# Edge network: some source rows fetched one by one on SyncE's queue, more columns copied on VectorE and ScalarE

## The chip, the cores and the metric

The kernel runs on one core of one Trainium2 chip. A core has five engines that run their own instruction streams: TensorE (PE in the profile, with its weight loads as PEld), VectorE (DVE), ScalarE (ACT), GpSimd (POOL) and SyncE (SP). Each has a sequencer that reads its stream in order, waits on semaphores and hands work to the engine; PEq, SPq and so on in the profile are these sequencers. DMAs are issued by SP, ACT or POOL and run on 16 shared DMA engines. SBUF is on-chip memory of 128 partitions, PSUM is where TensorE writes.

The metric is device time in microseconds (us). The kernel before takes 1879.1 us, the median of three runs (1875.58 to 1879.48).

## The reference

A graph has 12500 nodes with 64 features, and 212500 edges sorted by their destination, each with 32 features of its own. One layer computes a message for each edge from source, destination and edge features, sums messages by destination, updates the nodes and normalises:

```
msg_in = concatenate([nodes[src], nodes[dst], edge_features], axis=-1)   # 64 + 64 + 32
messages = relu(msg_in @ mW1 + mb1) @ mW2 + mb2                          # hidden size 128
aggregated = segment_sum(messages, dst, num_segments=12500)
upd_in = concatenate([nodes, aggregated], axis=-1)
update = relu(upd_in @ uW1 + ub1) @ uW2 + ub2
out = layernorm(nodes + update)
```

Everything is float32. The features of the source nodes must be fetched by index, in no order; the destinations of neighbouring edges lie close together.

## The kernel before, in words

**Groups and steps.** The edges are cut into tiles of 128 (P), and three tiles (TG) make a group; there are 554 groups (G). The main loop makes one step for each group k, numbered 0 to 553. One step's TensorE work is software-pipelined over groups: the transposes of group k (`turn`, L378), the hidden product of group k - 2 (`hidden`, L404) and the sums of group k - 4 (`sums`, L431, and every fourth step the counts, L442). In the last ten steps (SHORT) these stand in steps of their own. The first of TensorE's instructions in a step carries all the waits of the step.

**How the source features come in.** There are two ways.

- *Gathered.* `gather` (L164 to L175) issues on POOL one indirect DMA for each tile. It brings 128 rows of x (64 numbers each) to the 128 partitions of a tile in a ring `own.s` of 20 groups (RING). It is called 16 groups ahead (AHEAD), and waits until the group that used the ring's place before has been transposed. TensorE turns the tile over (`turn`), and ScalarE copies the result from PSUM to the matrix `own_st` (L389).
- *Copied as columns.* The kernel also holds x transposed in SBUF (`xc`, one column for each node). For the first tile of some groups (`COPIED`) nothing is gathered. Instead VectorE and ScalarE copy one column after another from `xc` to `own_st`, at an address that comes from a register (`fetch`, L565 on VectorE and L567 on ScalarE, 64 partitions by 4 bytes). From step 18 (BEGIN) to step 543 each step copies 44 columns: on VectorE 12 and 8 (VCOLS), on ScalarE 12 and 12 (ACOLS). Each such part is preceded by a load of its addresses into registers (`registers`, L546, a TENSOR_LOAD on the engine's own sequencer). The addresses come to SBUF eight steps at a time (`indexes`, L525, on SP), and VectorE scales them (`addresses`, L531). Where a tile is copied, ScalarE's copy from PSUM is in two pieces.

**The other work of a step.** VectorE takes the maximum with zero of the hidden product (L415), adds the sums into a window of 32 nodes of `agg` (L458, at an address from a register) and every fourth step the counts (L463), and writes the one-hot placement of a later group (`onehot`, L366). SP loads, for each group, a window of 32 projected destination rows as part of the hidden product's weights (`window`, L358, at a register address, four groups ahead), for each four groups the edge features (`inputs`, L316), and writes finished output (L516). In the first 25 steps parts of x and of the projected table also pass (L225, L226, L340 to L344). About every 22 steps a block of 512 nodes is complete, and its update runs in six pieces spread over following steps (L474 to L511).

**What sets the order.** The order of instructions on each engine is that of the program as written; no planner moves them. In a step, VectorE's first load of registers is recorded ahead of the addition L458, by a small list: `between.append(lambda: registers(k, 0))` before the step, and in `add`, `if between: between.pop()()`. Then come the step's additions, `fetch(0)` (the first part's columns), `window`, `onehot`, and for each later part its `registers` and `fetch`, and last the gather of group k + 16. Each DMA on SP uses one of eight semaphores in turn, and an instruction that reuses a semaphore waits for the DMA that had it before.

Of the kernel before, what the change touches and what calls it, by code (L numbers as in the profile page):

```python
# [10 lines left out]
F32 = mybir.dt.float32  # L11
BF16 = mybir.dt.bfloat16
I32 = mybir.dt.int32
# [3 lines left out]
ET = mybir.EngineType  # L17
# [15 lines left out]
G = (E + GE - 1) // GE  # L33
SB = 4
AHEAD = 16
RING = AHEAD + 4
BLOCKS = 3
NW = 2 * SB
COUNT = 96
# [9 lines left out]
TIMES = 4  # L49
BEGIN = 18  # L50
CHECKED = 8
VCOLS = (12, 8)
ACOLS = (12, 12)
COLS = sum(VCOLS + ACOLS)
SPAN = 8


def tiles_of(g):

    n = min(GE, E - g * GE)  # L60
    return [min(P, n - j * P) for j in range((n + P - 1) // P)]
# [23 lines left out]
COPIED = []  # L85
while BEGIN - (-P * (len(COPIED) + 1) // COLS) < G - SHORT:
    COPIED.append(BEGIN - (-P * (len(COPIED) + 1) // COLS))


class Own:  # L90
# [24 lines left out]
def ordered(ctx: ExitStack, tc: tile.TileContext, a, own, ok):  # L115
# [21 lines left out]

    loads, places_by, copy_by, relu_by, sums_by, wm_by, turn_by = ({} for _ in range(7))
    efs_by, hidden_by, counted_by = {}, {}, {}
    columned = set(COPIED)  # L140

    def after(first, *others):

# [20 lines left out]
    def gather(g):  # L164
        s = own.s[g % RING]
        loads[g] = [
            nc.gpsimd.indirect_dma_start(  # L167
                out=s[:p, j, :D], out_offset=None, in_=x[:, :],
                in_offset=bass.IndirectOffsetOnAxis(
                    ap=src_sb[:p, g * TG + j : g * TG + j + 1], axis=0),  # L170
            )
            for j, p in enumerate(tiles_of(g)) if j or g not in columned
        ]
        for i in loads[g]:
            after(i, *([turn_by[g - RING]] if g >= RING else []))  # L175

# [93 lines left out]
    wc = const.tile([H, H], F32, name="wc")  # L270

    starts, rows_at, indices, columns_by = {}, {}, {}, {}
    by_dst = dram.tile([NP, H], F32, name="by_dst")
    written = []

# [9 lines left out]

    def ordered_edges():

        off = temp.tile([P, G * TG], F32, name="off")
        valid = temp.tile([P, 2], F32, name="valid")
        nc.vector.tensor_scalar(off, dlc, 0.0, 0.0, ALU.is_ge, ALU.add, accum_out=valid[:, 0:1])  # L290
        nc.vector.tensor_scalar(off, dlc, W - 1.0, 0.0, ALU.is_le, ALU.add, accum_out=valid[:, 1:2])
        low = temp.tile([1, G], F32, name="low")
        opens = [0, *(closes for *_, closes in PLAN)]
        for (base, *_), g0, g1 in zip([*PLAN, (N,)], opens, [*opens[1:], G]):
            if g0 < g1:
                nc.vector.memset(low[:, g0:g1], float(base))
        wrong = temp.tile([1, 2, G], F32, name="wrong")
        nwrong = temp.tile([1, 1], F32, name="nwrong")
        first_f = temp.tile([1, G], F32, name="first_f")
        nc.vector.tensor_copy(first_f, first_i[0:1, :])  # L300
        nc.vector.tensor_tensor(wrong[:, 0], first_f, low, ALU.is_lt)
        nc.vector.tensor_tensor(wrong[:, 1], first_f, high, ALU.is_gt)
        nc.vector.tensor_reduce(nwrong, wrong, mybir.AxisListType.XY, ALU.add)
        vps = ups.tile([H, CH], F32, name="u_ps")
        for i in range(2):
            nc.tensor.matmul(vps[0:1, 0:1], ones[:, 0:1], valid[:, i : i + 1], start=i == 0,
                             stop=i == 1)
        nv = temp.tile([1, 1], F32, name="nv")
        nc.vector.tensor_tensor(nv, vps[0:1, 0:1], nwrong, ALU.subtract)
        nc.vector.tensor_scalar(ok, nv, float(E + P * G * TG), None, ALU.is_equal)  # L310
# [52 lines left out]
    def onehot(g):  # L363
        if g >= G:
            return
        places_by[g] = nc.vector.tensor_tensor(  # L366
            own.s[g % RING][:, :, D:], iota.unsqueeze(1).to_broadcast([P, TG, W]),
            dlc[:, g * TG : (g + 1) * TG].unsqueeze(2).to_broadcast([P, TG, W]), ALU.is_equal,
        )
        after(places_by[g], *([counted_by[g - RING]] if g >= RING else []))  # L370

    def turn(g, ps):


        s = own.s[g % RING]
        xt = ps[0][: D + W, :GE]
        did = [
            nc.tensor.transpose(xt[:, j * P : j * P + p], s[:p, j, :], ident[:p, :p])  # L378
            for j, p in enumerate(tiles_of(g))
        ]  # L380

        def copy(step):
            t, c, n = columns(g)
            turn_by[g] = step
            whole = [(slice(D + W), slice(n))]
            apart = [(slice(D, D + W), slice(P)), (slice(D + W), slice(P, n))]
            copies = [
                ordered_by_steps(
                    after(nc.scalar.activation(t[r, c : c + n][:, m], xt[r, m], AF.Copy), step))  # L389
                for r, m in (apart if g in columned else whole)  # L390
            ]
            if g >= BLOCKS * SB:
                after(copies[0], hidden_by[g - BLOCKS * SB])
            copy_by[g] = copies
            return copies

        return did, [*loads.pop(g), places_by[g]], copy

    def hidden(g, ps):
        t, c, n = columns(g)  # L400
# [24 lines left out]
    def sums(g, ps):  # L425
        h, s = own.h[g % NH], own.s[g % RING]
        sizes = tiles_of(g)
        sg = ps[2][:, : TIMES * W].rearrange("p (t w) -> p t w", w=W)
        did = []
        for j, p in enumerate(sizes):  # L430
            did.append(nc.tensor.matmul(  # L431
                sg, h[:p, j, :],
                s[:p, j, D:].unsqueeze(1).to_broadcast([p, TIMES, W]),
                start=j == 0, stop=j == len(sizes) - 1))
        counts = []
        if g % SB == SB - 1 or g == G - 1:
            g0 = g // SB * SB
            whole = [q for q in range(g0, g + 1) if tiles_of(q) == [P] * TG]
            at_ps = ps[2][0:1, TIMES * W :][:, : SB * W].rearrange("o (q w) -> o q w", w=W)
            first_s = g0 % RING  # L440
            for j in range(TG):
                did.append(nc.tensor.matmul(  # L442
                    at_ps[:, : len(whole)], own.one,
                    own.ring[:, first_s : first_s + len(whole), j, D:],
                    start=j == 0, stop=j == TG - 1))
            if len(whole) < g + 1 - g0:
                for j, p in enumerate(sizes):
                    did.append(nc.tensor.matmul(
                        at_ps[:, len(whole)], own.one[:p], s[:p, j, D:],
                        start=j == 0, stop=j == len(sizes) - 1))  # L450
            counts = [(q, at_ps[:, q - g0]) for q in range(g0, g + 1)]

        def add(step):
            sums_by[g] = step
            at = bass.ds(starts[g], W)
            if between:
                between.pop()()
            did = [after(nc.vector.tensor_tensor(agg[:, at], sg[:, 0, :], agg[:, at], ALU.add),  # L458
                         step)]
            for q, counted in counts:  # L460
                counted_by[q] = step
                count = xc[COUNT : COUNT + 1, bass.ds(starts.pop(q), W)]
                did.append(after(nc.vector.tensor_tensor(count, counted, count, ALU.add), step))  # L463
            return did

        return did, [*relu_by[g], *copy_by[g]], add
# [53 lines left out]
    def indexes(i):  # L520

        n = min(SPAN * COLS, P * len(COPIED) - i * SPAN * COLS)
        if n > 0:
            indices[i] = ixp.tile([1, SPAN * COLS], I32, name="index")
            nc.sync.dma_start(indices[i][:, :n], a["src_copied"][:, i * SPAN * COLS :][:, :n])  # L525
# [27 lines left out]
    def fetch(*parts):  # L553

        for part in parts:
            engine, c0, v = held.pop(part, (None, 0, ()))
            for q, at in enumerate(v, c0):
# [8 lines left out]
                else:  # L566
                    by[engine] = nc.scalar.activation(o, x_at, AF.Copy)  # L567
                ordered_by_steps(after(by[engine],
                                       *([hidden_by[g - BLOCKS * SB]] if new else [])))

    waiting = [(closes, update(base, p, n)) for base, p, n, closes in PLAN]
    now = []

# [37 lines left out]
    for g in range(SB):  # L611
        window(g)
    indexes(0)
    made = summed = 0
    between, held = [], {}

    for k in range(G):
        if k < BITS:
# [11 lines left out]
        if k % SB == 1:  # L630
            places(k // SB + 1)
        if k < G - SHORT:
            between.append(lambda: registers(k, 0))
            step((turn, k), *([(hidden, k - 2)] if k > 1 else []),
                 *([(sums, k - 4)] if k > 3 else []))
            made, summed = max(0, k - 1), max(0, k - 3)
            if between:
                between.pop()()
            fetch(0)
        else:  # L640

            step((turn, k))
            for _ in range(2):
                if summed < made:
                    step((sums, summed))
                    summed += 1
            for _ in range(2):
                if made <= k:
                    step((hidden, made))
                    made += 1  # L650
        window(k + SB)
        onehot(k + LEAD)
        if k < G - SHORT:
            for part in range(1, len(VCOLS + ACOLS)):
# [338 lines left out]
```

## Time and profile before

| | |
|---|---|
| median of three runs | 1879.1 us (1875.58 to 1879.48) |
| profiled execution: its own time | 1872.44 us |
| its span in the profile | 1870.6 us |
| granted TensorE clock, mean | 0.952 |
| busy: ACT, DVE, POOL, PE | 1558.7, 1452.9, 1400.1, 1302.0 us |
| gathers on POOL (L167) | 1481, mean 945 ns |
| columns on ACT (L567), on DVE (L565) | 12560, 10480 |
| DMAs of SP's windows (L358) | 554, 16 KB each |
| data moved by DMA | 104.10 MB, mean 56 GB/s |

The profile shows one execution. A busy time is the time in which the engine ran at least one instruction; register loads, semaphores and the issuing of DMAs are not in it. A group's row reads: line, engine, operation, output and input tiles, count, then busy time in us and mean ns of one instruction, then the idle time of the engine just before these instructions and what ended most of it. A row of waits reads: who waited, for whom, us in total, times, longest. A row that begins with "L... SPq" (a source's instructions) gives count, then shortest, median and longest duration in ns, then the first and the last start in us. A row of the timeline gives the start and the duration in us, then the instruction; equal instructions close together are merged with their count.

### The profile page before, as it was taken

The numbers are of one execution on the slowest core, as the hardware profiler recorded it, in microseconds if no ns is written. First come the engines' busy times: TensorE is split into PE (matmuls) and PEld (weight loads), VectorE is DVE, ScalarE is ACT, GpSimd is POOL, SyncE is SP. The second block draws the span as 40 slices with busy tenths as digits, with TensorE's granted clock in tenths as the row PEclk, the third lists the DMA queues.
The fourth block names the chain that finished last, engine by engine and source line by source line (L and its number), as shares of the span: only waits on it lengthen the run. The fifth ranks groups of instructions, "written<-read, shape, count | busy, mean of one in ns | idle before, by whom it ended". The sixth has DMA issues, their size and how long they took to land. (4 is left out here: it accounts for less than half of the span.)

```text
span 1870.6 us, 55967 instructions
## 1 busy us (share of the span) xinstructions
PE 1302.0 (70%) x9839; PEld 1139.3 (61%) x9839; DVE 1452.9 (78%) x13141; ACT 1558.7 (83%) x13374; POOL 1400.1 (75%) x1488
## 2 busy tenths in 40 slices
PE   1777777677767667677676776776767767667676
PEld 0676666666666556566665666665656656556665
DVE  1338888899897888877887878888878888888773
ACT  5249999999998888888888888888888888888871
POOL 7777777777777777777777777777777777777774
PEclk9889999999999998998999998999998999999999
DMA  4543222222222222222222222222222222222221
GB/s 93 138 123 75 54 54 54 51 54 53 52 54 48 50 52 49 50 49 45 54 52 47 52 46 54 48 51 48 53 46 53 45 54 51 48 53 48 50 49 26
DMA packets 112796, 104.10 MB, mean 56 GB/s; under 512 B 51586, under 2 KB 82960, under 8 KB 112432
## 3 DMA queue, kind: packets, MB, share of 16 engines
q0 software_dynamic: 47392, 48.60, 14.8%
q1 hardware_dynamic: 64196, 51.35, 10.0%
q14 instruction: 280, 2.29, 0.4%
q8 instruction: 84, 1.38, 0.3%
q10 hardware_dynamic: 844, 0.48, 0.1%
HBM read 90.61 MB, written 9.62 MB: 54 GB/s over the span
## 5 line engine op out<-in xcount | busy, mean ns | idle before, releaser
L167 POOL DMA_INDIRECT own_s<-in_x,src_sb x1481 | 1399.4, 945 | 452.5 <-issue 342.9
L567 ACT ACTIVATE own_st<-own_xc 64x4 uint8 x12560 | 1265.6, 192 | 60.2 <-issue 52.2
L565 DVE COPY own_st<-own_xc 64x4 uint8 x10480 | 884.5, 190 | 17.3 <-issue 9.2
L378 PE MATMUL own_ps<-own_ident,own_s 128*96 128x128 f32 x1661 | 294.1, 288 | 488.7 <-DMA own_s<-in_x,src_sb 164.0
L378 PEld LDWEIGHTS own_ps<-own_ident,own_s 128*96 128x96 f32 x1661 | 169.1, 131 | 593.5 <-issue 291.0
L431 PE MATMUL own_ps<-own_s,own_h 128*128 128x128 f32 x3322 | 490.3, 287 | 1.2 <-DVE own_h L415 0.6
L404 PE MATMUL own_ps<-own_wm,own_st 128*128 128x128 f32 x3322 | 485.5, 285 | 0.0
L415 DVE TENSOR_SCALAR own_h<-own_ps 128x384 f32<-128x384 f32 x553 | 302.1, 547 | 185.5 <-PE own_ps L442 84.7
L431 PEld LDWEIGHTS own_ps<-own_s,own_h 128*128 128x128 f32 x3322 | 443.3, 203 | 2.3 <-DVE own_h L415 1.2
L404 PEld LDWEIGHTS own_ps<-own_wm,own_st 128*128 128x128 f32 x3322 | 437.8, 201 | 1.8 <-issue 1.2
L389 ACT ACTIVATE own_st<-own_ps 96x384 f32<-96x384 f32 (+2 forms) x734 | 294.2, 401 | 167.5 <-PE own_ps L442 81.6
L458 DVE TENSOR_TENSOR own_agg<-own_ps,own_agg 128x32 f32 x554 | 105.8, 191 | 170.6 <-DVE own_h L415 90.4
L366 DVE TENSOR_TENSOR own_s<-iota,dlc 128x96 f32<-128x96 f32 x554 | 136.2, 247 | 0.3 <-issue 0.2
L442 PE MATMUL own_ps<-own_s,own_one 128*1 128x128 f32 x834 | 120.6, 283 | 0.0
L463 DVE TENSOR_TENSOR own_xc<-own_ps,own_xc 1x32 f32 x554 | 101.9, 184 | 18.5 <-DVE own_xc L463 1.8
L442 PEld LDWEIGHTS own_ps<-own_s,own_one 128*1 128x1 f32 x834 | 60.2, 85 | 35.7 <-issue 3.6
L340 PE MATMUL u_ps<-w1b,own_xc 65*128 65x128 f32 x196 | 33.4, 323 | 58.1 <-ACT t L343 38.8
L340 PEld LDWEIGHTS u_ps<-w1b,own_xc 65*128 65x128 f32 x196 | 29.1, 227 | 62.3 <-ACT t L343 42.1
L343 ACT ACTIVATE t<-u_ps 128x512 f32<-128x512 f32 (+1 forms) x25 | 14.7, 588 | 58.2 <-DMA by_dst<-t 37.9
L487 PE MATMUL u_ps<-same,own_xc 65*128 65x64 f32 (+1 forms) x196 | 37.0, 271 | 1.5 <-ACT u L480 1.4
L489 PE MATMUL u_ps<-u,u 128*128 128x64 f32 (+1 forms) x196 | 38.0, 276 | 0.0
L487 PEld LDWEIGHTS u_ps<-same,own_xc 65*128 65x128 f32 (+1 forms) x196 | 29.7, 191 | 2.3 <-ACT u L480 2.2
(62 smaller groups left out, 257.1 us busy)
## 6 DMA issues: line engine op xcount, KB each, us to landing
own_st<-in_efT SPq DMA_DIRECT2D x138, 192.0 KB
own_s<-in_x,src_sb POOLq DMA_INDIRECT x1481
own_wm<-by_dst SPq DMA_DIRECT2D x554, 16.0 KB
by_dst<-t SPq DMA_DIRECT2D x24, 256.0 KB
out<-o SPq DMA_DIRECT2D x24, 128.0 KB
own_xc<-in_xT SPq DMA_DIRECT2D x12, 179.2 KB
index<-in_src_copied SPq DMA_DIRECT2D x65, 1.4 KB
dlc_i<-in_dst_cols SPq DMA_DIRECT2D x1, 831.0 KB
```

Source lines behind the costliest of these rows:

```text
L167: nc.gpsimd.indirect_dma_start(out=s[:p, j, :D], out_offset=None, in_=x[:, :], in_offset=bass.IndirectOffsetOnAxis(ap=src_sb[:p, g * TG + ...
L366: places_by[g] = nc.vector.tensor_tensor(own.s[g % RING][:, :, D:], iota.unsqueeze(1).to_broadcast([P, TG, W]), dlc[:, g * TG : (g + 1) * ...
L378: nc.tensor.transpose(xt[:, j * P : j * P + p], s[:p, j, :], ident[:p, :p])
L389: after(nc.scalar.activation(t[r, c : c + n][:, m], xt[r, m], AF.Copy), step))
L404: nc.tensor.matmul(pre[:p, j, :], t[:, c + j * P : c + j * P + p], wm[g % NW], start=True, stop=True)
L415: relu_by[g] = [nc.vector.tensor_scalar(h, pre, 0.0, None, ALU.max)]
L431: did.append(nc.tensor.matmul(sg, h[:p, j, :], s[:p, j, D:].unsqueeze(1).to_broadcast([p, TIMES, W]), start=j == 0, stop=j == len(sizes) - 1))
L442: did.append(nc.tensor.matmul(at_ps[:, : len(whole)], own.one, own.ring[:, first_s : first_s + len(whole), j, D:], start=j == 0, stop=j == ...
L458: did = [after(nc.vector.tensor_tensor(agg[:, at], sg[:, 0, :], agg[:, at], ALU.add), step)]
L463: did.append(after(nc.vector.tensor_tensor(count, counted, count, ALU.add), step))
L565: by[engine] = nc.vector.tensor_copy(o, x_at)
L567: by[engine] = nc.scalar.activation(o, x_at, AF.Copy)
```

## The change

Four things are changed together.

1. *Rows on SP.* From step 18 on, SP fetches six rows of x in each step (ROWS_A_STEP), each by its own DMA of 256 bytes in two halves, into one partition of the third tile of a group. 24 such tiles (`BY_ROWS`) are filled over 512 steps, one after another, 128 rows each; the last row of a tile is issued two steps (ROW_LEAD) before the tile's transposes. POOL no longer gathers these tiles. The node numbers come to SBUF 96 at a time (`row_indexes`), and every second step SP loads 12 of them into registers (`row_numbers`); a row's address is computed from its register. In SP's order the rows stand behind the step's window load.
2. *More columns.* VCOLS becomes 8, 8, 8 and ACOLS 12, 8, 8: 52 columns a step instead of 44, and three loads of registers on each of the two engines instead of two. 213 tiles are copied instead of 180.
3. *VectorE's first load behind the additions.* The list `between` is gone; `registers(k, 0)` now stands after the step's additions, just before `fetch(0)`.
4. *Memory.* The ring of gathered groups has 24 places instead of 20, and a temporary `off` of the start shares the memory of `dlc_i`.

On POOL 1424 gathers remain of 1481. SP issues 3072 row DMAs more.

```
-RING = AHEAD + 4
+RING = 24
-VCOLS = (12, 8)
-ACOLS = (12, 12)
+VCOLS = (8, 8, 8)
+ACOLS = (12, 8, 8)
+ROWS_A_STEP = 6
+PAIR = 2 * ROWS_A_STEP
+ROW_SPAN = 8 * PAIR
+ROW_LEAD = 2
+BY_ROWS = []
+while True:
+    last = BEGIN + (P * (len(BY_ROWS) + 1) - 1) // ROWS_A_STEP
+    if last + ROW_LEAD >= G - SHORT:
+        break
+    BY_ROWS.append(last + ROW_LEAD)
...
-            for j, p in enumerate(tiles_of(g)) if j or g not in columned
+            for j, p in enumerate(tiles_of(g))
+            if (j or g not in columned) and (j < TG - 1 or g not in by_rows)
...
-        off = temp.tile([P, G * TG], F32, name="off")
+        off = dlc_i.bitcast(F32)
...
-        return did, [*loads.pop(g), places_by[g]], copy
+        return did, [*loads.pop(g), *rows_by.pop(g, []), places_by[g]], copy
...
-            if between:
-                between.pop()()
...
+    def row_indexes(i):
+        n = min(ROW_SPAN, P * len(BY_ROWS) - i * ROW_SPAN)
+        if n > 0:
+            row_index[i] = ixp.tile([1, ROW_SPAN], I32, name="row_index")
+            nc.sync.dma_start(row_index[i][:, :n], a["src_rows"][:, i * ROW_SPAN :][:, :n])
+
+    def row_numbers(k):
+        q, odd = divmod(k - BEGIN, 2)
+        if k < BEGIN or odd:
+            return
+        i, b = divmod(q * PAIR, ROW_SPAN)
+        n = min(PAIR, P * len(BY_ROWS) - q * PAIR)
+        if n > 0:
+            _, v = nc.values_load_multi_w_load_instructions(
+                row_index[i][0:1, b : b + n], engines=[ET.SP], min_val=0, max_val=N - 1,
...
+            fetched.extend(enumerate(v, q * PAIR))
+        if b == ROW_SPAN - PAIR:
+            row_indexes(i + 1)
+
+    def row_fetch():
+        for q, node in [fetched.pop(0) for _ in fetched[:ROWS_A_STEP]]:
+            g, p = BY_ROWS[q // P], q % P
+            i = nc.sync.dma_start(
+                own.s[g % RING][p : p + 1, TG - 1, :D].rearrange("p (a b) -> p a b", a=2),
+                x[bass.ds(node, 1), :].rearrange("p (a b) -> p a b", a=2))
+            after(i, *([turn_by[g - RING]] if g >= RING and not p else []))
+            rows_by.setdefault(g, []).append(i)
...
         if k < G - SHORT:
-            between.append(lambda: registers(k, 0))
             step((turn, k), *([(hidden, k - 2)] if k > 1 else []),
                  *([(sums, k - 4)] if k > 3 else []))
-            if between:
-                between.pop()()
+            registers(k, 0)
             fetch(0)
...
         window(k + SB)
+        row_numbers(k)
+        row_fetch()
         onehot(k + LEAD)
```

More of the change, by code (lines that the diff above doesn't have):

```diff
@@ L139, in ordered @@
     efs_by, hidden_by, counted_by = {}, {}, {}
-    columned = set(COPIED)
+    columned, by_rows = set(COPIED), set(BY_ROWS)
     def after(first, *others):
@@ L272, in ordered @@
     starts, rows_at, indices, columns_by = {}, {}, {}, {}
+    rows_by, row_index = {}, {}
     by_dst = dram.tile([NP, H], F32, name="by_dst")
@@ L569, in fetch @@
                                        *([hidden_by[g - BLOCKS * SB]] if new else [])))
+    def row_indexes(i):
[3 more added lines that the diff above has]
+            nc.sync.dma_start(row_index[i][:, :n], a["src_rows"][:, i * ROW_SPAN :][:, :n])
+    fetched = []
+    def row_numbers(k):
[7 more added lines that the diff above has]
+                row_index[i][0:1, b : b + n], engines=[ET.SP], min_val=0, max_val=N - 1,
+                skip_runtime_bounds_check_because="a source is one of the nodes",
+            )
+            fetched.extend(enumerate(v, q * PAIR))
[9 more added lines that the diff above has]
+            rows_by.setdefault(g, []).append(i)
     waiting = [(closes, update(base, p, n)) for base, p, n, closes in PLAN]
@@ L613, in ordered @@
     indexes(0)
+    row_indexes(0)
     made = summed = 0
-    between, held = [], {}
+    held = {}
     for k in range(G):
@@ L974 @@
         "src_copied": np.concatenate([v["src"][g * GE :][:P] for g in COPIED])[None],
+        "src_rows": np.concatenate([v["src"][g * GE + GE - P :][:P] for g in BY_ROWS])[None],
         "dst_cols": padded(v["dst"], G * TG * P, -1).reshape(G * TG, P).T,
```

## The prediction

> **What bounds the kernel now.** I first read the page's busy shares and costliest groups, and then the waits of GpSimd (POOL), whose group has the most idle time before it.
>
> ```profile
> span 1870.6 us, 55967 instructions
> PE 1302.0 (70%) x9839; PEld 1139.3 (61%) x9839; DVE 1452.9 (78%) x13141; ACT 1558.7 (83%) x13374; POOL 1400.1 (75%) x1488
> L167 POOL DMA_INDIRECT own_s<-in_x,src_sb x1481 | 1399.4, 945 | 452.5 <-issue 342.9
> ```
> ```profile
> POOL own_s L167 <- issue: 342.9, 1125, 0.3
> POOL own_s L167 <- DMA own_s<-in_x,src_sb: 85.3, 280, 0.3
> POOL own_s L167 <- PE own_ps L431: 19.2, 63, 0.3
> ```
>
> ACT has the highest busy share, but POOL is the engine that never rests: its 1481 gathers take 1399.4 us, and the 452.5 us between them come in pieces of at most 0.3 us. One gather costs (1399.4 + 452.5) / 1481 = 1.250 us, and these two together are 1851.9 of 1870.6 us.
>
> A share over the whole span hides two stages, so I asked for the busy time in two stretches and counted steps by L415, which runs once a step (rows: first both stretches, then L415, VectorE's and ScalarE's columns and ScalarE's copies in 200 to 400 us, last L415 in 700 to 1700 us).
>
> ```profile
> core 0: us, PE busy (x) PEld busy (x) DVE busy (x) ACT busy (x) POOL busy (x), PEclk, DMA share, GB/s
> 200.00:400.00 200.00, 148.57 (x1171) 130.45 (x1172) 178.52 (x1666) 192.77 (x1733) 151.24 (x161) 0.98 0.25 53
> 700.00:1700.00 1000.00, 698.88 (x5229) 609.89 (x5230) 807.50 (x7436) 871.11 (x7659) 755.98 (x801) 0.94 0.24 50
> ```
> ```profile
> L567 ACT ACTIVATE own_st<-own_xc 64x4 uint8 x1636 | 164.3, 193 | 3.6 <-issue 3.0
> L565 DVE COPY own_st<-own_xc 64x4 uint8 x1347 | 113.7, 189 | 2.3 <-issue 1.4
> L415 DVE TENSOR_SCALAR own_h<-own_ps 128x384 f32<-128x384 f32 x68 | 36.9, 543 | 0.4 <-issue 0.2
> ```
> ```profile
> L415 DVE TENSOR_SCALAR own_h<-own_ps 128x384 f32<-128x384 f32 x302 | 165.2, 547 | 74.9 <-PE own_ps L442 56.7 <-PE own_ps L431 17.1 <-issue 0.2
> ```
>
> From 700 us on a step takes 1000 / 302 = 3.31 us, POOL's pace (801 gathers, 2.65 a step, at 1.250). Earlier, while POOL's lead of 16 groups lasts, a step takes 200 / 68 = 2.94 us and ScalarE is busy 192.77 of 200. So POOL leads by little: ScalarE stands 0.37 us a step behind it.
>
> SyncE (SP) issues all other loads. Its own waits show how idle it is.
>
> ```profile
> SPq L316 <- PE own_ps L431: 521.4, 108, 6.7
> SPq L516 <- DVE o L511: 264.7, 23, 13.7
> SPq L358 <- PE own_ps L442: 240.2, 95, 5.7
> SPq L525 <- DVEq L546: 129.1, 50, 4.1
> ```
>
> These four alone are 1155 us of waiting: SP has much free time, and the change spends it.
>
> **The change, part by part.**
>
> *Gathers.* Columns go from 44 to 52 a step: floor(526 x 52 / 128) = 213 tiles against 180. Rows fill 24 tiles. 33 + 24 = 57 gathers go, 57 x 1.250 = 71.3 us of POOL. On the path that is the gain only while POOL stays the bound.
>
> *Columns and registers.* ScalarE gets 4 columns more a step at 164.3 / 1636 = 0.100 us: +0.40. Its busy time was 192.77 / 68 = 2.835 a step, so 3.24 gapless and, at the same 96% busy, 3.36 us. VectorE gets 4 more at 113.7 / 1347 = 0.084: 178.52 / 68 = 2.63 becomes 2.96, and it loads registers three times (8, 8, 8) where it did twice (12, 8).
>
> ```profile
> L546 DVEq TENSOR_LOAD <-index x1048: 591/843/1125, 123.6 to 1817.6; - x175
> L546 ACTq TENSOR_LOAD <-index x1047: 549/782/1358, 123.6 to 1814.8; - x175
> L525 SPq DMA_DIRECT2D index<-in_src_copied x66: 269/270/308, 43.2 to 1778.4; - x66
> ```
> ```profile
> DVE own_agg L458 <- DVE own_h L415: 90.4, 229, 0.8
> DVE own_agg L458 <- issue: 54.6, 139, 0.8
> ```
>
> An 8-register load is near the least of VectorE's row (0.591 us) and a 12-register one near 0.843; three of 0.6 are 0.36 more than 0.84 + 0.6, partly beside the columns. Moving the first load behind the additions removes what stands before L458, (90.4 + 54.6) / 554 = 0.26 us a step, and puts a like stall before the first column: I count zero, bounds -0.26 and +0.36. All this lies beside SP's longer step (below); with that cover gone, the step is ScalarE's 3.36, or up to 0.36 more if VectorE cannot hide the third load.
>
> *Ring of 24, the shared buffer.* The ring could save POOL's waits for TensorE, 19.2 us at most, and only if POOL is the bound; `off` in `dlc_i` changes two early instructions' address. Both: nothing.
>
> *Rows.* In 512 steps (18 to 529) SP issues six DMAs more, each with its address work, and every second step loads 12 registers. No one-row DMA at a register address is in the trace; the nearest is the window load L358, also at a register address (timeline of SP at the start where nothing holds it, then sources L358, L353, L316, L516 and L266).
>
> ```profile
> 41.25 1.90 SPq L358 DMA_DIRECT2D own_wm<-by_dst  x4
> 43.20 0.31 SPq L525 DMA_DIRECT2D index<-in_src_copied  x1
> ```
> ```profile
> L358 SPq FUSED_REGOPS  x554: 37/37/51, 39.8 to 1830.3; - x185
> L358 SPq MOVE own_wm<-by_dst x554: 29/29/38, 41.2 to 1830.4; - x185
> L358 SPq DMA_DIRECT2D own_wm<-by_dst x554: 315/316/1517, 41.3 to 1830.6; - x185
> ```
> ```profile
> L353 SPq TENSOR_LOAD <-start_i x139: 293/315/743, 39.2 to 1827.3; - x139
> ```
> ```profile
> L316 SPq DMA_DIRECT2D own_st<-in_efT x139: 321/322/740, 22.1 to 1826.0; - x139
> ```
> ```profile
> L516 SPq DMA_DIRECT2D out<-o x24: 409/414/415, 191.5 to 1859.9; - x24
> ```
> ```profile
> L266 ACTq DMA_DIRECT2D same<-in_ub x1: 287/287/287, 14.5 to 14.5; - x1
> ```
>
> Four window loads in a row take (43.20 - 41.25) / 4 = 0.49 us each, of which address work, register move and DMA are 0.037 + 0.029 + 0.316 and three gaps the rest, 0.036 each. A DMA that writes one partition costs SP 0.270 (L525) and ScalarE 0.287 (L266, also 256 bytes); I take 0.28, because these two have the row's shape. A row then costs 0.49 - 0.316 + 0.28 = 0.454 us. Bounds: 0.270 below; above, the dearest issue of SP's steady stage, 0.414.
>
> SP's step: six rows 2.72; window load 0.49 and a semaphore, 0.52; row numbers as ScalarE's 12 registers, (0.78 + 0.04) / 2 = 0.41; window registers (0.315 + 0.04) / 4 = 0.09; features (0.32 + 0.06) / 4 = 0.10; both index loads 0.33 / 8 + 0.31 / 16 = 0.06; output about 0.47 / 23 = 0.02. Sum 3.92 us, more than POOL's 3.31 and ScalarE's 3.36. Behind the rows in SP's order stand the window and feature loads that TensorE's hidden product needs, and TensorE's transposes of a row tile need rows issued two steps earlier. It can run a few steps ahead between row tiles, and each row tile (one in 21 steps) brings it back to SP's pace. So SP sets the steps.
>
> A row's DMA also waits for the one eight before it on SP's semaphores. At 0.5 us apiece that one is 4 us old, and a gather lands in 2.4, so I count nothing; a landing beyond 4 us would add to every step.
>
> ```profile
> 133.44 0.30 SPq L525 DMA_DIRECT2D index<-in_src_copied  x1
> ```
> ```profile
> 1830.08 2.39 DMA own_s<-in_x,src_sb
> ```
>
> *Sum.* The rows of step 18 stand just before this index load: start 133.4. 512 x 3.92 = 2007 gives 2140. The last rows land 2.4 us later, 2143, and step 531 begins. Twelve steps at 3.36 are 40. From the start of the last column step to the end it is now 1870.6 - 1814.8 = 55.8, at least 30 gathers' pace (37.5 us); with gathers long ready I take 45 (bounds 30 and 56). Span 2228; the profiled execution's 1872.44 is 1.84 longer than its span, so **2230 us**. That execution is 0.35% under the median of 1879.1 of the runs shown (1875.58 to 1879.48), so a timed run may read some 8 us more.
>
> [...] L358's and L525's rows say that a DMA costs SP 0.27 to 0.32 us. [...]
>
> **The rivals.**
>
> *Rows cheap, ScalarE binds.* If SP can issue a row in under 0.36 us (its step then is under 3.36), ScalarE's 28 columns decide: 123.6 + 525 x 3.36 + 55.8 + 1.8 = 1945 us, 1882 if it ran gapless. For it: the bare instructions of a row sum to 0.35. Against: the measured gaps. [...]
>
> *POOL stays the bound (faster).* If SP's and ScalarE's steps both stay under POOL's new pace, (2.65 - 57 / 526) x 1.250 = 3.18 us, all 57 gathers count: 1872.4 - 71.3 = 1801. For it: POOL binds now. Against: ScalarE's gapless 3.24 is already above.
>
> *Rows dearer.* A row's two 128-byte pieces might cost what the output's issue does, 0.414: 2230 + 512 x 6 x 0.134 = 2642.
>
> **How the numbers follow.** Forecast 0.75 (own range 2199 with 0.270 a DMA, up to 2600), ScalarE binds 0.10, POOL stays 0.05, dearer rows 0.10. The range 1940 to 2600 takes in ScalarE's 1945 and leaves out the last two, 0.15. About 0.2% is what this measurement can tell from none. Faster 0.05 (POOL's rival), same 0.01, slower 0.94.
>
> **What would show it.** Right: SP's own waits fall to almost nothing; rows issue every 0.45 us; between 700 and 1700 us a step takes 3.9 us, POOL waits for TensorE and is busy 2.54 x 0.945 = 2.4 us of it, ScalarE's busy share falls to about 83% (3.24 of 3.92); L458 no longer waits for a load; 1424 gathers. Wrong: SP still waits long for TensorE while ScalarE is above 95% busy (second case), or POOL's gaps stay at 0.3 us (third). What would break the forecast is the price of a row's issue: each 0.01 us is 31 us of the total.

## The result and the profile after

The changed kernel takes 2261.47 us (median of four runs, 2257.49 to 2264.81). The kernel before, timed beside it, takes 1877.74 us (1875.58 to 1879.48). The ratio is 1.2043, 95% interval 1.2019 to 1.2068: one fifth slower. The prediction was 2230 us in a range of 1940 to 2600, with 0.94 on slower. Some kernels of the experiments were timed where the kernel before itself took 2436 to 2465 us; each ratio is to a kernel before timed beside it, and what is said of times rests on the timings beside 1873 to 1876 us where there is one.

First the page of the kernel after: span, busy shares, and the rows of the gathers and the columns.

```profile
span 2259.6 us, 70816 instructions
PE 1406.7 (62%) x9839; PEld 1236.7 (55%) x9839; DVE 1671.8 (74%) x15253; ACT 1754.6 (78%) x15519; POOL 1349.6 (60%) x1431
L177 POOL DMA_INDIRECT own_s<-in_x,src_sb x1424 | 1348.8, 947 | 806.6 <-issue 378.9
L577 ACT ACTIVATE own_st<-own_xc 64x4 uint8 x14672 | 1456.3, 192 | 55.3 <-issue 40.8
```

POOL has 57 gathers less and its idle time has grown from 452.5 to 806.6 us: it is no longer the engine that never rests. No engine is above 78% busy. SP's own waits of the kernel after:

```profile
SPq L370 <- DMA by_dst<-t: 46.5, 24, 3.7
SPq L526 <- DVE o L521: 31.1, 8, 12.1
SPq L526 <- DVE own_agg L468: 26.0, 2, 25.7
```

These are the three largest. Before, SP waited 521.4, 264.7 and 240.2 us for TensorE and VectorE; now it waits for almost nothing, and the others wait for it (waits of the kernel after):

```profile
PE own_ps L390 <- DMA own_s<-in_x: 233.2, 22, 18.4
POOL own_s L177 <- PE own_ps L443: 206.8, 102, 14.1
DVE own_st L575 <- issue: 214.0, 732, 0.7
```

The first row is the one to learn from. TensorE's transposes wait once for each of the 24 row tiles, 6.5 to 18.4 us at a time, for the last row of the tile (the row has 22 of these waits; the other two, of 8.3 and 10.1 us, the profile puts down to instructions of VectorE): that is where the whole core is brought back to SP's pace. POOL then waits for TensorE to free ring places (second row).

The steady stage, 700 to 1700 us, kernel after (busy time by engine, then L427, which runs once a step):

```profile
700.00:1700.00 1000.00, 623.59 (x4405) 548.02 (x4404) 783.77 (x7289) 825.01 (x7503) 613.33 (x648) 0.87 0.20 42
```
```profile
L427 DVE TENSOR_SCALAR own_h<-own_ps 128x384 f32<-128x384 f32 x254 | 138.1, 544 | 78.4 <-PE own_ps L443 48.4 <-PE own_ps L454 29.7 <-issue 0.2
```

254 steps in 1000 us are 3.94 us a step, against 3.31 before. ScalarE is busy 82.5% of it, so there is room on every engine whose busy time the page counts. TensorE's granted clock is 0.87 here and was 0.94 in this stretch before, but TensorE is busy 62% of the stretch and waits for rows, so its clock does not set the step. SP's work is issuing, which the page does not count as busy; it has to be read from the sources (kernel after: count, then shortest, median and longest ns, first and last start) and from SP's timeline.

```profile
L610 SPq FUSED_REGOPS  x3072: 37/37/42, 134.6 to 2164.9; - x192
L610 SPq MOVE own_s<-in_x x3072: 29/29/29, 134.7 to 2165.0; - x192
L610 SPq DMA_DIRECT2D own_s<-in_x x3072: 224/228/279, 134.8 to 2165.0; - x192
L598 SPq TENSOR_LOAD <-row_index x256: 745/762/953, 133.8 to 2158.6; - x128
L365 SPq TENSOR_LOAD <-start_i x139: 300/558/743, 39.4 to 2219.7; - x139
```
```profile
1000.28 2.28 SPq L610 DMA_DIRECT2D own_s<-in_x  x6
1002.66 0.33 SPq L328 DMA_DIRECT2D own_st<-in_efT  x1
1003.17 0.32 SPq L370 DMA_DIRECT2D own_wm<-by_dst  x1
1004.66 2.33 SPq L610 DMA_DIRECT2D own_s<-in_x  x6
```

From the first row to the last, SP needs (2164.9 - 134.6) / 512 = 3.965 us a step, and the step of the whole kernel is the same to 1%. In the trace SP's instructions fill the stretch from 1000 to 1200 us without a gap above 0.35 us. Nor is it the landing of the rows that SP stands for: its list of waits has no row of L610.

### The profile page after: what moved, and what is told of

Same layout as the page of the kernel before. It is cut to its first block, busy times and chain, and to the rows that moved or that the text cites. A ratio compares the mean times of both kernels' runs of the same rounds, so it can differ in the third digit from the quotient of the medians.

```text
span 2259.6 us, 70816 instructions
## 1 busy us (share of the span) xinstructions
PE 1406.7 (62%) x9839; PEld 1236.7 (55%) x9839; DVE 1671.8 (74%) x15253; ACT 1754.6 (78%) x15519; POOL 1349.6 (60%) x1431
## 5 line engine op out<-in xcount | busy, mean ns | idle before, releaser
L177 POOL DMA_INDIRECT own_s<-in_x,src_sb x1424 | 1348.8, 947 | 806.6 <-issue 378.9
L577 ACT ACTIVATE own_st<-own_xc 64x4 uint8 x14672 | 1456.3, 192 | 55.3 <-issue 40.8
L575 DVE COPY own_st<-own_xc 64x4 uint8 x12592 | 1117.4, 185 | 269.6 <-issue 214.0
L390 PE MATMUL own_ps<-own_ident,own_s 128*96 128x128 f32 x1661 | 317.0, 306 | 751.8 <-issue 244.4
L390 PEld LDWEIGHTS own_ps<-own_ident,own_s 128*96 128x96 f32 x1661 | 183.4, 139 | 856.9 <-issue 572.1
L443 PE MATMUL own_ps<-own_s,own_h 128*128 128x128 f32 x3322 | 529.1, 302 | 5.3 <-DVE own_h L427 2.7
L416 PE MATMUL own_ps<-own_wm,own_st 128*128 128x128 f32 x3322 | 528.3, 302 | 0.0
L427 DVE TENSOR_SCALAR own_h<-own_ps 128x384 f32<-128x384 f32 x553 | 301.2, 545 | 265.7 <-PE own_ps L443 135.7
L443 PEld LDWEIGHTS own_ps<-own_s,own_h 128*128 128x128 f32 x3322 | 481.9, 218 | 7.9 <-DVE own_h L427 4.4
L416 PEld LDWEIGHTS own_ps<-own_wm,own_st 128*128 128x128 f32 x3322 | 481.6, 218 | 2.4 <-issue 1.2
L468 DVE TENSOR_TENSOR own_agg<-own_ps,own_agg 128x32 f32 x554 | 97.0, 175 | 11.6 <-PE own_ps L443 6.2
L484 PE MATMUL u_ps<-own_agg,wc 128*128 128x512 f32 (+1 forms) x50 | 27.3, 628 | 22.8 <-DVE own_agg L468 22.8
```

Source lines behind the costliest of these rows:

```text
L177: nc.gpsimd.indirect_dma_start(out=s[:p, j, :D], out_offset=None, in_=x[:, :], in_offset=bass.IndirectOffsetOnAxis(ap=src_sb[:p, g * TG + ...
L416: nc.tensor.matmul(pre[:p, j, :], t[:, c + j * P : c + j * P + p], wm[g % NW], start=True, stop=True)
L427: relu_by[g] = [nc.vector.tensor_scalar(h, pre, 0.0, None, ALU.max)]
L443: did.append(nc.tensor.matmul(sg, h[:p, j, :], s[:p, j, D:].unsqueeze(1).to_broadcast([p, TIMES, W]), start=j == 0, stop=j == len(sizes) - 1))
L575: by[engine] = nc.vector.tensor_copy(o, x_at)
```

## The experiments

The theory is that SP's issue time sets the step: six row DMAs a step put more on SP than POOL or ScalarE need. The rivals are that the 52 columns set it, that the order of VectorE's load matters, or that a row's DMA is dear for its two pieces.

### The rows alone, 44 columns a step

The changed kernel with the columns and the load order of before:

```
-VCOLS = (8, 8, 8)
-ACOLS = (12, 8, 8)
+VCOLS = (12, 8)
+ACOLS = (12, 12)
...
-            registers(k, 0)
+            if between:
+                between.pop()()
```

> Six rows a step as in the changed kernel, but 44 columns and VectorE's first load where they were before. Theory (SyncE's issue sets the steps): SP's work a step is untouched at 3.96 us, so the time stays within 20 us of the changed kernel, about 2250 us, a little less only because the steps after the last row run at 2.94 instead of 3.36 us. Rival (the eight more columns and the third register load bind): without them the time falls to about 1872 - 24 x 1.25 = 1842 us.

Measured beside a kernel before of 2435.58 us: 3070.49 us, ratio 1.2618 (1.2527 to 1.2709). The repetition:

> The same kernel as rows6_cols44, now beside a kernel before at its usual time. Theory (SP's issue sets the steps): SP's 3.96 us a step whatever the columns, about 2250 us, ratio near 1.20. Rival (the eight more columns and the third load bind): 1842 us, ratio 0.98.

Measured: 2234.03 us against 1876.06, ratio 1.1893 (1.1872 to 1.1914). Eight columns a step less, one register load less on each engine, and only 27 us of the 385 us are gone (I had allowed 20). Its sources and steady stage:

```profile
L612 SPq DMA_DIRECT2D own_s<-in_x x3072: 224/228/306, 132.6 to 2150.9; - x192
```
```profile
700.00:1700.00 1000.00, 591.64 (x4463) 520.15 (x4464) 679.76 (x6321) 725.41 (x6507) 630.06 (x667) 0.86 0.17 43
```
```profile
PE own_ps L390 <- DMA own_s<-in_x: 431.8, 23, 20.7
```

ScalarE is busy 73% now and VectorE 68%, yet SP's step is (2150.9 - 132.6) / 512 = 3.94 us, 0.02 under the changed kernel's. With the other engines ahead of SP, TensorE's wait for the rows is longer (431.8 instead of 233.2 us). So the rows alone, on SP, make the step. The two spans differ by 24.5 us. Of these, 14 lie up to the last row: (2165.0 - 134.8) - (2150.9 - 132.6) = 11.9, and the later start, 2.2. The rest lies behind the last row. So a step with rows was not quite untouched by the columns, as I had expected.

### The columns alone

The changed kernel with no row tile; the gathers that they replace are back:

```
-    if last + ROW_LEAD >= G - SHORT:
+    if last + ROW_LEAD >= 0:
```

> The 52 columns, the three loads and the load behind the additions, without any row. Theory: SP is idle again and the columns decide. ScalarE's 28 columns give 3.36 us a step and 1945 us, 1882 us if it runs gapless; VectorE's third load could add up to 0.36 us a step, 2135 us at most. Rival (POOL still binds, and the 33 gathers that go count in full): 1872 - 33 x 1.25 = 1831 us. If the rows had no part in the slowdown: 2261 us.

Measured beside a kernel before of 2435.58 us: 2524.02, ratio 1.0363 (1.0301 to 1.0426), and again:

> The same kernel as cols52_only. Theory: without rows SP is idle and ScalarE's 28 columns decide: 3.36 us a step, 1945 us (1882 gapless), up to 2135 if VectorE's third load adds 0.36 us a step. Rival (POOL binds): 1831 us. Rows without a part in it: 2261 us.

Measured: 2083.46 us, ratio 1.112 (1.107 to 1.117), between ScalarE's 1945 us and the 2135 that I had allowed for VectorE's third load. The columns are not harmless: alone they cost 11%, although 33 gathers are saved. In 700 to 1700 us of this kernel (steady stage, L427, VectorE's columns; then SP's first wait):

```profile
700.00:1700.00 1000.00, 647.20 (x4796) 564.80 (x4795) 853.03 (x7919) 907.05 (x8149) 678.70 (x717) 0.94 0.18 45
```
```profile
L427 DVE TENSOR_SCALAR own_h<-own_ps 128x384 f32<-128x384 f32 x276 | 149.9, 543 | 0.5 <-issue 0.4
L575 DVE COPY own_st<-own_xc 64x4 uint8 x6624 | 592.1, 186 | 135.7 <-issue 108.5
```
```profile
SPq L328 <- PE own_ps L443: 573.2, 107, 7.5
```

A step takes 1000 / 276 = 3.62 us. L427 never waits for TensorE (0.5 us in all), so it is VectorE that is always behind: it runs 853.03 / 276 = 3.09 us a step, and of the rest 135.7 / 276 = 0.49 us stands before its columns, where it has just loaded registers, now three times a step. ScalarE, at 907.05 / 276 = 3.29 us a step, stands near. SP is idle again (573.2 us in one row). Part 2 of the change thus has a bound of its own at 3.62 us, which SP's 3.97 hides in the changed kernel.

### VectorE's load behind the additions, alone

The kernel before without `between`; `registers(k, 0)` just before `fetch(0)`:

```
-            between.append(lambda: registers(k, 0))
...
-            if between:
-                between.pop()()
+            registers(k, 0)
```

> The kernel before with VectorE's first register load moved behind the additions and nothing else. Theory: the stall moves from the addition to the first column and POOL binds as before, so no change: within 0.3% of the kernel before; VectorE's idle time before the addition (145 us) shows up before the columns instead. Rival (the addition's delay held up TensorE): faster by up to 0.26 us in the 170 steps before POOL's lead is used up, 44 us.

Measured beside 2435.58 us: 2445.78, ratio 1.0043 (1.0011 to 1.0076). Again:

> The same kernel as load_after_add. Theory: POOL binds, the stall of 145 us before the addition shows up before the first column, and the time stays within 0.3% of the kernel before. Rival: faster by up to 44 us.

Measured: 1876.31 us, ratio 0.9999 (0.9989 to 1.0008). Moving the load is neutral. The stall has only changed its place; of the kernel with the load moved, the wait before VectorE's columns is now

```profile
DVE own_st L563 <- issue: 188.8, 389, 1.1
```

where before there stood 90.4 + 54.6 = 145.0 us ahead of L458 and 9.2 us ahead of the columns.

### The row as one piece

```
-                own.s[g % RING][p : p + 1, TG - 1, :D].rearrange("p (a b) -> p a b", a=2),
-                x[bass.ds(node, 1), :].rearrange("p (a b) -> p a b", a=2))
+                own.s[g % RING][p : p + 1, TG - 1, :D], x[bass.ds(node, 1), :])
```

> The changed kernel with each row's DMA as one piece of 256 bytes instead of two of 128. Theory (SP's issue sets the steps, and a row's price is the sequencer's work on one DMA instruction, 0.228 us, whatever its pieces): DMA and time unchanged, within 1% of the changed kernel's own ratio of 1.204 to the kernel before. Rival (the two pieces are what a row costs, in issue or in landing): a DMA at 0.20 us or less, and 512 x 6 x 0.03 = 92 us less.

Measured beside a kernel before of 2465.11 us: 3073.54, ratio 1.2459 (1.2339 to 1.2578). The sources of this kernel:

```profile
L610 SPq DMA_DIRECT2D own_s<-in_x x3072: 3/228/800, 193.0 to 2971.9; - x192
```

The median issue is 228 ns, the same as with two pieces in the changed kernel. The kernel with rows alone, two pieces and 3070.49 us, has 228 ns in its profile too. How the row is cut costs SP nothing. The ratio of 1.2459 lies outside the 1% around 1.204 that I expected, but it does not speak of the pieces: the rows alone went from 1.1893 beside 1876.06 us to 1.2618 beside 2435.58 us, and the changed kernel itself was not timed beside such a kernel before. So the issue's price is shown, the effect on the whole time is not.

### Rows in bursts, with rests between

If SP is late only while it issues rows, a tile's 128 rows could be issued in 22 steps and the next 44 left free. This is the kernel with rows alone, PERIOD = 66 and ON = 22, so that 8 tiles come by rows instead of 24:

```
+PERIOD = 66
+ON = 22
...
-    last = BEGIN + (P * (len(BY_ROWS) + 1) - 1) // ROWS_A_STEP
+    last = BEGIN + PERIOD * len(BY_ROWS) + ON - 1
...
-        if k < BEGIN or odd:
+        if k < BEGIN or at >= ON or at % 2 or i >= len(BY_ROWS):
```

> 44 columns and the old order; six rows a step only in 22 of every 66 steps, so eight row tiles instead of 24. Theory: in the 22 steps SP's 3.96 us against the 3.31 us of a step puts TensorE 14 us behind, within POOL's lead of 16 groups; in the 44 steps after it SP needs 1.2 us and the engines 2.94, which makes up 44 x 0.37 = 16 us. POOL binds on average and eight gathers less give 1872 - 10 = 1862 us. Rival (a row costs time wherever it stands): 8 x 22 x 0.65 = 114 us more, about 1977 us.

Measured beside 2435.58 us: 2631.39, ratio 1.0802 (1.0732 to 1.0872). Again:

> The same kernel as rows6_pause66_cols44. Theory: 14 us of delay in each 22 steps with rows, made up in the 44 steps without; POOL binds with eight gathers less, 1862 us. Rival (a row's step costs its excess wherever it stands): 8 x 22 x 0.65 = 114 us more, 1977 us minus the gathers' 10.

Measured: 1893.29 us (1891.17 to 1897.44), ratio 1.0091 (1.0074 to 1.0109). Neither number came, but the two are not equally far: of the 115 us that the rival wanted over the theory's 1862, 31 appeared. In this kernel POOL's row is, as before,

```profile
L178 POOL DMA_INDIRECT own_s<-in_x,src_sb x1473 | 1395.2, 947 | 454.8 <-issue 324.6 <-DMA own_s<-in_x,src_sb 107.1 <-PE own_ps L444 15.4
```
```profile
PE own_ps L391 <- DMA own_s<-in_x: 104.3, 6, 18.9
```

POOL never stands: its 1473 gathers go at (1395.2 + 454.8) / 1473 = 1.256 us, so SP's delay does not hold them up. But TensorE is held eight times, once for each row tile, for 15.6 to 18.9 us (counted in the trace; the row above has the six that the profile puts down to the rows' DMAs, 104.3 us). After the first burst the balance of burst and rest is as the theory said: each 66 steps take 210 to 216 us, where POOL's pace in the kernel before makes 218 to 219. What the theory left out is the start, where SP has other DMAs too: the 41st step (by L428, in the kernel before L415) begins at 231.6 us instead of 202.8. At the end of the list TensorE is behind: from the start of the last gather to the end pass 38.7 us, where the kernel before needs 18.1. Eight saved gathers (10 us) do not pay for that. So SP's delay is forgiven as far as POOL's lead reaches, and what is not made up again appears in the tail. That the first burst makes most of it was not tried apart.

### More columns without a third load on VectorE

If POOL binds the kernel before, then taking gathers from it without loading SP should pay. Three kernels without rows, in the load order of before, tried to find such a split of columns. The first, 50 columns in two loads on each engine:

```
-VCOLS = (12, 8)
-ACOLS = (12, 12)
+VCOLS = (12, 12)
+ACOLS = (14, 12)
```

> No rows; 50 columns a step (VectorE 12 and 12, ScalarE 14 and 12) with two register loads on each engine and the old place of VectorE's first load. Theory: where nothing but the engines' work counts, POOL still binds: 25 gathers less are 31 us, 1872 - 31 = 1841 us; ScalarE's 26 columns need (2.835 + 0.20) / 0.964 = 3.15 us a step, under POOL's 3.26. Rival (VectorE's 24 columns bind at 2.63 + 0.34 + 0.3 of stalls = 3.3 us or more): no faster than before, 1880 to 1900 us.

Measured: 2921.47 us against 1873.27, ratio 1.561 (1.5577 to 1.5643). Instead of 2% faster, it is half as long again. The sources of its register loads:

```profile
L558 DVEq TENSOR_LOAD <-index x1050: 841/1032/3314, 122.1 to 2867.5; - x175
L558 ACTq TENSOR_LOAD <-index x1050: 495/1683/3561, 122.9 to 2862.8; - x175
```

Loads that took 0.84 and 0.78 us in the kernel before now take up to 3.6 us. The only new size is 14 registers, so the next two kernels changed that: one has 14 and nothing else that is new (46 columns: 12 and 8, 14 and 12), one has no load above 12 (48 columns: 12 and 10, 12, 8 and 6).

```
+VCOLS = (12, 8)
+ACOLS = (14, 12)
```

> No rows by number, 46 columns a step: VectorE 12 and 8 as before, ScalarE 14 and 12, so the only new thing is one load of 14 registers on ScalarE. Theory (the 14-register load is what made 50 columns slow): far above the kernel before, 2300 to 2950 us, with ScalarE's loads of 1.2 us and more. Rival (it was VectorE's second load of 12 registers, or the two together): POOL's 8 or 9 gathers fewer, 9 x 1.250 = 11 us off, about 1865 us.

```
+VCOLS = (12, 10)
+ACOLS = (12, 8, 6)
```

> No rows by number, all gathers of the kernel before, but 48 columns a step: VectorE 12 and 10, ScalarE 12, 8 and 6, no load longer than 12 registers, loads where the kernel before has them. Theory (POOL binds the kernel before; the long time of 50 columns came from its register loads, and ScalarE's step stays under POOL's 3.28 to 3.31 us): 17 gathers fewer, 17 x 1.250 = 21 us off, about 1855 us. Rival 1 (two 12-register loads on VectorE or three loads on ScalarE are already the longer ring: ScalarE 3 x 0.55 + 26 x 0.19 and more): steps of 3.4 to 3.6 us, 1900 to 2000 us. Rival 2 (any departure from loads of 8 and 12 breaks the pace as 50 columns did): above 2300 us.

Measured beside a kernel before of 2437.73 us: 46 columns 2850.79, ratio 1.1699 (1.1655 to 1.1744); 48 columns 3764.12, ratio 1.5438 (1.538 to 1.5495). Both are far slower, and the size of 14 cannot be the cause of the second. Their sources, 46 columns first:

```profile
L558 DVEq TENSOR_LOAD <-index x1047: 595/902/3076, 178.0 to 2791.7; - x175
L558 ACTq TENSOR_LOAD <-index x1046: 779/1994/3608, 178.6 to 2792.3; - x175
```
```profile
L558 ACTq TENSOR_LOAD <-index x1567: 1317/1745/3240, 180.0 to 3709.6; - x196
L558 DVEq TENSOR_LOAD <-index x1046: 843/1066/1509, 180.0 to 3702.3; - x175
```

In the 48-column kernel no load on ScalarE is under 1.317 us, though its sizes 12 and 8 are old ones, while VectorE's are all normal. What differs between them is where the load begins. The addresses lie one behind the other, four bytes each; with 48 a step and parts of 12, 10, 12, 8 and 6, VectorE's loads begin at places 0 and 12 and ScalarE's at 22, 34 and 42 of every step. VectorE's are multiples of four, ScalarE's are not. With 46 or 50 a step every second step begins off a multiple of four. I sorted the loads of these three kernels by size and by that (medians in us, counted in the trace; the three kernels agree to 0.03 where they share a kind, although the one with 50 columns was timed beside 1873.27 us and the others beside 2437.73):

| load | first place a multiple of 4 | not a multiple of 4 |
|---|---|---|
| VectorE, 8 registers | 0.60 | 1.85 |
| VectorE, 10 | 1.07 | none |
| VectorE, 12 | 0.85 | 2.73 |
| ScalarE, 6 | none | 1.33 |
| ScalarE, 8 | 0.55 (kernel after) | 1.74 |
| ScalarE, 12 | 0.79 | 2.60 |
| ScalarE, 14 | 1.23 | 3.02 |

There is no overlap between the columns: of each size every load falls with its group, up to single ones that are longer or shorter. Off a multiple of four (16 bytes) a register costs 0.22 us ((2.73 - 1.85) / 4); on it, 0.06 ((0.85 - 0.60) / 4); and two registers left over behind the last four cost about 0.22 each again (14 against 12 on ScalarE: 0.44). That goes far to account for these three kernels: in the 50-column one VectorE's two loads take 2 x 2.73 us every second step, and in the 48-column one ScalarE's three take 2.60 + 1.74 + 1.33 = 5.67 us of a step of (3709.6 - 180.0) / 525 = 6.72. It also answers my two expectations: the size of 14 is not what broke the pace, and neither are two loads of 12. That 46 columns came out in the theory's range of 2300 to 2950 us is luck, then: another cause gave the number. The places were found by sorting, not by a run that moves them alone, and no such run was made. It is not that every second step is slow for another reason: with 46 columns ScalarE's loads of 12 are long in the even steps, and VectorE's loads and ScalarE's of 14 in the odd ones. All places off a multiple of four are two past one; odd places do not occur. All parts of the changed kernel (8, 8, 8, 12, 8, 8 and SP's 12) are multiples of four, so its result does not contain this cost: in its trace the medians are 0.595 us (VectorE, 8), 0.547 (ScalarE, 8), 0.782 (ScalarE, 12) and 0.762 (SP, 12).

What stays open is the case that these three were meant for: 48 columns as 12, 12, 12 and 12, where all loads begin on a multiple of four. It was not tried, so that POOL's pace is worth 1.25 us for each gather in the kernel before rests on the profile, not on an experiment. No kernel that was run beats the kernel before.

## Why the prediction was right, point by point

**POOL's 57 gathers are no longer on the path.** Right. POOL's idle time rose to 806.6 us, and it waits for TensorE in pieces of up to 14.1 us where it never waited longer than 0.3. It is busy 613.33 / 254 = 2.41 us a step, as predicted.

**SP sets the step.** Right, by the signs named beforehand (SP's waits nearly gone, a step of 3.94 us, ScalarE at 82.5%, and the addition, now L468, idle 0.0 us before it between 700 and 1700 us) and by the experiment: without the added columns SP's step stays at 3.94 us. The range alone would not tell, since it also took in ScalarE's 1945. That a row's DMA would not wait for the one eight before it was right too (no row of L610 in SP's waits).

**The price of a row.** Too high, and the largest error of the sum. I took 0.454 us, with 0.28 for the DMA between bounds of 0.270 and 0.414. The row's DMA costs SP 0.228 us, under the lower bound: it is cheaper than any DMA that the trace before showed. Nor was the index load's 0.270, from which I took the price, a fixed one: in the kernel after, the same load (L535) has a median of 0.234. Why is open. Six rows in a burst take 2.28 us by the timeline, so one follows the other after (2.28 - 0.228) / 5 = 0.41 us. Counted over all 512 steps of the trace, with the gap behind each instruction, rows are 2.50 us a step, not 2.72. Of the 0.41 more than 0.18 is not the DMA but what stands around it: 0.037 and 0.029 us for two register instructions, and gaps.

**The rest of SP's step.** Too low, by a little more: 3.965 - 2.50 = 1.46 us against the 1.20 that I summed. Counted in the same way, row numbers are 0.45 instead of 0.41 (the loads have a median of 0.762, but a mean of 0.844). The window's register load has a median of 0.558 where before it was 0.315, so 0.15 a step instead of 0.09. The window is 0.56 instead of 0.52, features and index loads are 0.01 dearer each, and the output is 0.06 instead of 0.02, most of it waiting. And there is a pause that I did not know of, of 0.34 us after every 128 instructions of SP, 0.05 us a step (below). That the two errors cancel is luck; the sum of 3.92 against 3.965 is better than its parts.

**The start, the end.** The rows begin at 134.6 (133.4 predicted). Behind the last row there are 2259.6 - 2165.0 = 94.6 us, where I had 88. So of the 31 us that the measured span is over the predicted 2228, some 24 come from the steps (512 x 0.045 and the start), and 7 from the end.

**Columns and registers.** The direction was right, the engine that I put first was not. I put the step without SP's cover at ScalarE's 3.36 us "or up to 0.36 more if VectorE cannot hide the third load". Alone the columns make 3.62, VectorE's number, 0.26 over ScalarE's and within that allowance. So the rival "ScalarE binds", 1945 us, had the wrong engine and a price too low: with cheap rows the time would have been nearer to 2080.

**Moving the load: nothing.** Right to a tenth of a per cent (0.9999), with the stall in front of the columns, as predicted.

**The ring and the shared buffer** were not tried apart. The kernel with bursts has both and is 0.9% slower in all, so they are not what costs 20%.

**What a DMA costs SP.** L358's and L525's rows of the trace before had 0.27 to 0.32 us; the 3072 row DMAs took SP 0.228 us in the median. From row to row it is 0.41 us, the address work included. Six times 0.41 us are 62% of a step of 3.97 us: with this many small rows, issuing them set the step.

**Rows dearer** (0.414 a DMA) did not come; in one piece or two the row has the same price, 0.228 us in the median.

## What to carry to other kernels

An engine that "only issues" has a pace too, and the busy shares do not show it: count its issues a step with the distance from one to the next, which for these rows is 0.41 us, 1.8 times the duration of the DMA instruction itself. Exchanging 24 gathers (24 x 1.250 = 30 us of POOL; the other 33 went to columns) for 3072 single-row DMAs plus their address work (512 x 2.50 = 1280 us of SP) is only free as long as SP's step fits into the step of the others, and it did not: 3.965 us against the 3.62 of the columns alone. Before a load of registers is added, or its size changed, look where it begins: here a load that did not begin at a multiple of four addresses (16 bytes) took 2.5 to 3.3 times as long (the table above).

## What the runs showed of the hardware that I had not expected

- Register loads by place: 0.85 us for 12 registers on VectorE when the first is at a multiple of four places (16 bytes) in the index tile, 2.73 us when it is two places past one (ScalarE: 0.79 and 2.60).
- A DMA of one row of 256 bytes at a register address costs SP's sequencer 0.228 us, less than the window's 0.321 in the same kernel. The index load took 0.234 in this kernel and 0.270 in the kernel before.
- SP's stream pauses for about 0.34 us after every 128 of its instructions: in 1000 to 1200 us of the changed kernel there are nine such gaps, 20.7 to 22.3 us apart, with 128 instructions from each to the next. The page lists instructions as a DMA queue of its own (below: packets, MB, share of 16 engines; 8.2 KB a packet). In this stretch a packet of that queue starts 0.97 to 1.35 us after the start of each of the nine gaps (counted in the trace); what makes SP pause was not shown.

```profile
q14 instruction: 396, 3.24, 0.5%
```
